# Turning the three-row maxima of an attention step by a transposing DMA instead of by TensorE

## The chip, the core and the metric

The kernel runs on one core of one Trainium2 chip. The metric is the device time of one execution in microseconds (us). Engines are named as in the profile: PE is TensorE (PEld its weight loads), DVE is VectorE, ACT is ScalarE, POOL is GpSimd, SP is SyncE, whose queue issues nearly all DMAs here. L560 means line 560 of the kernel before.

## The reference

An attention layer with a conditioning token and a residual. `x` is 8 x 512 x 512 (batch, sequence, model), with 16 heads of 32.

```python
Q = split_heads(x @ Wq.T + bq); K = ... Wk, bk; V = ... Wv, bv
tQ = split_heads(cond @ Wq.T + bq); tK = split_heads(cond @ Wk.T + bk)
scores = einsum('bhqd,bhkd->bhqk', Q + tQ, K + tK) / sqrt(32)
out = einsum('bhqk,bhkd->bhqd', softmax(scores), V)
return x + merge_heads(out)
```

All inputs and the output are float32.

## The kernel before, in words

**Steps.** The work is cut into 32 steps `t = 4*b + g` (T = 32): one batch `b` and one group `g` of four heads, whose 4 x 32 channels fill the 128 partitions. A step has four stages, and the loop at L796 writes out their order by hand for PE, ACT, DVE and POOL (a manual schedule), for t = 0 to 28. The last three steps have an order of their own (L904 onwards). The DMAs on SP are not in that manual schedule: the framework places them in SP's queue.

**Two passes over the scores.** A softmax needs the row maxima of the scores with queries on the partitions, but the probabilities are wanted with keys on the partitions, so that they can be multiplied with V without a transpose. So each step computes its scores twice. `row_max` (L482) has PE make scores with queries on partitions (L499), and DVE reduces them to negated maxima `nmax`, 128 x 4 x 4 (L490, L508). ACT then runs over the same scores once more for the sums of the exponentials (`denominators`, L518). Later `exponentials` (L555) has PE make the scores with keys on partitions (L563), with the negated maxima added in the same accumulation: L560 multiplies three rows of `maxT` by ones. ACT takes the exponential of that (L574).

**Three rows.** `maxT` holds, for each head, the negated maxima as three bfloat16 rows whose sum is the float32 value. `split_max` (L526) makes the three parts on POOL, in four small instructions (L532 to L535), into `split`, a 128 x 512 bfloat16 tile with the queries on partitions, used in turn from two buffers. `transpose_max` (L539) turns it: four PE transposes of 128 x 128 (L544) into one PSUM bank, and one copy from there into `maxT` (L550), which DVE does in the loop.

**Stages of iteration t.** Each begins with `exponentials(t, kc)` for one quarter `kc` of the keys, goes on with a `row_max` of the next step or, in the last stage, of the step after it, and ends with a share of other PE work:

- stage q: `row_max(t+1, 1)`, then a share of the q projection of the next batch (L406),
- stage w: `row_max(t+1, 2)`, then the probabilities times V of step t-1 (L579), and the result of step t-1 goes out by way of DVE (L635), POOL (L636, L637) and SP (L640),
- stage k: `row_max(t+1, 3)`, which completes the maxima of step t+1; `split_max(t+1)` on POOL; a share of the k projection; `load_residual(t+1)` (L165 on SP, L173 on POOL),
- stage v: `row_max(t+2, 0)`, then a share of the v projection (L403), in whose middle a callback `small` (L842) calls `transpose_max(t+1, ...)`.

The next iteration opens with `exponentials(t+1, 0)`, the first reader of `maxT[t+1]`. The letters q, w, k and v are used for the stages below.

**What orders the work.** Each engine runs its instructions in the written order; semaphores tie the engines together. PSUM has eight banks, dealt out to the stages by the table `TURNS`: per stage four banks for the exponentials (and then the projection), and four for the row maxima. Each transpose used one of these for a moment (index 1 or 2 of its stage). `split` has two buffers and `maxT` has two. On SP the DMAs of an iteration stand in this order: four loads of `x` blocks (L151), which wait for DVE; four stores of a result (L640), which wait for POOL's L637; four loads of a residual block (L165), one iteration ahead of their use.

Of the kernel before, what the change touches and what calls it, by code (L numbers as in the profile page):

```python
# [10 lines left out]
BF16 = mybir.dt.bfloat16  # L11
# [6 lines left out]
def kernel(  # L18
# [38 lines left out]
    nc = tc.nc  # L57
    P = 128
    B, S, D = x.shape
# [5 lines left out]
    NS = S // P  # L65
    NC = D // P
    SCALE = 1.0 / math.sqrt(HD)
    T = B * G
# [8 lines left out]
    op = ctx.enter_context(tc.tile_pool(name="op", bufs=2))  # L77
# [34 lines left out]
    def banks(i, n=1):  # L112

        j = TURNS[turn[0]][i]
        if n == 1:
            return psum[:, j, :]
        k = TURNS[turn[0]][i + 1]
        return psum[:, j : k + 1 : k - j, :]

    def advance():  # L120
        turn[0] = {7: 0, len(TURNS) - 1: 4}.get(turn[0], turn[0] + 1)
# [37 lines left out]
    def load_residual(t):  # L159

        b, g = divmod(t, G)
        if turned_by_vector(t):
            xr[t] = op.tile([P, NB, BL], F32, tag="xr", name=f"xr_{t}", bufs=3)
            for h in range(HG):
                nc.sync.dma_start(  # L165
                    xr[t][h * BL : (h + 1) * BL], spread(x[b], g * P + h * BL)
                )
            bias = bvs[:, g, :].unsqueeze(1).broadcast_to([P, NB, BL])
        else:

            xr[t] = xT[b][:, g, :]
            bias = bvl.broadcast_to([P, S])
        nc.gpsimd.tensor_tensor(xr[t], xr[t], bias, ALU.add)  # L173
# [62 lines left out]
    split = []  # L236
# [8 lines left out]
    for i in range(NS):  # L245
        r = slice(i * BL, (i + 1) * BL)
# [70 lines left out]
    def turn_x(n):  # L317
        b, cc = divmod(n, NC)
        if b >= B:
            return  # L320
        if cc == 0:
            xT[b] = xtp.tile([P, NC, S], F32, tag="xT", name=f"xT_{b}")
        nc.vector.transpose(xT[b][:, cc, :], xs[n].rearrange("p f i -> p (f i)"))
        load_block(n + NC)
# [106 lines left out]
    def first_products(n, b, u, dens, small, at, first=0):  # L431


        one_, two_ = banks(first), banks(at)
        c1, c12, c2, c22 = parts_of(n, b, u)
        m1 = c2[:, 0, :]
        product(n, b, u, 1, one_[:, :HS])
        nc.scalar.copy(m1, one_[:, :HS])
        dens()
        product(n, b, u, 6, two_[:, :HS])  # L440
        small()
        product(n, b, u, 2, two_[:, HS:], (0,))
        product(n, b, u, 7, one_[:, HS:])
        nc.vector.tensor_tensor(c12, two_[:, :HS], m1, ALU.add)
        nc.vector.tensor_tensor(c1[:, 0, :], two_[:, HS:], m1, ALU.add)
        plus(n, b, u, 1, c22, one_[:, HS:], c12)
# [18 lines left out]
    def project_pair(n, b, r, dens, small, at):  # L465

        if b >= B:
            dens()
            small()
        else:  # L470
            (first_products, other_products)[r % 2](n, b, r // 2, dens, small, at)
# [10 lines left out]
    def row_max(t, qc):  # L482
        if t >= T:
            return
        open_max(t)
        for j in range(HG):
            row_scores(t, qc, j, banks(HG + j))
        if t < T - 2 or t * NS + qc == T * NS - 1:
            for j in range(2):
                nc.vector.tensor_reduce(  # L490
                    nmax[t][:, qc, j : j + 1, 0], banks(HG + j), AX.X, ALU.max, negate=True
                )
        else:
            row_max_of(t, qc, 0, banks(HG, 2))
        row_max_of(t, qc, 1, banks(HG + 2, 2))
# [16 lines left out]
    def denominators(t, qc, prs=range(NP)):  # L512

        if t >= T - 2:
            return
        for j in [pr * 2 + i for pr in prs for i in range(2)]:
            dead = op.tile([P, S], F32, tag="dead", name=f"dead_{t}_{qc}_{j}")
            nc.scalar.activation(  # L518
                dead,
                banks(HG + j),  # L520
                AF.Exp,
                bias=nmax[t][:, qc, j, :],
                accum_out=sums[t][:, qc, j, :],
            )

    def split_max(t, on=nc.gpsimd):  # L526

        if t >= T:
            return
        m, sp = nmax[t], split[t % 2]  # L530
        rest = op.tile([P, NS, HG, 1], F32, tag="rest", name=f"rest_{t}")
        on.tensor_copy(sp[:, :, :, 0:1], m)  # L532
        on.tensor_tensor(rest, m, sp[:, :, :, 0:1], ALU.subtract)
        on.tensor_copy(sp[:, :, :, 1:2], rest)
        on.tensor_tensor(sp[:, :, :, 2:3], rest, sp[:, :, :, 1:2], ALU.subtract)  # L535

    maxT = {}

    def transpose_max(t, bank, copy=nc.vector.tensor_copy):  # L539
        if t >= T:  # L540
            return
        pt = bank.bitcast(BF16)
        for qc in range(NS):
            nc.tensor.transpose(  # L544
                pt[:, qc * P : (qc + 1) * P],
                split[t % 2][:, qc, :, :].rearrange("p h e -> p (h e)"),
                identb,
            )
        maxT[t] = op.tile([P, S], BF16, tag="maxT", name=f"maxT_{t}")
        copy(maxT[t], pt[:, :S])  # L550
# [4 lines left out]
    def exponentials(t, kc, at=None):  # L555

        bank = [psum[:, i, :] for i in at] if at else [banks(i) for i in range(HG)]
        for j in range(HG):
            r = slice(j * HD, j * HD + 3)
            nc.tensor.matmul(bank[j], onesb[r, :], maxT[t][r, :], start=True, stop=False)  # L560
        for j in range(HG):
            r = slice(j * HD, (j + 1) * HD)
            nc.tensor.matmul(  # L563
                bank[j],
                qkT["k", t][r, kc * P : (kc + 1) * P],
                qkT["q", t][r, :],
                start=False,
                stop=True,
            )
        for pr in range(NP):  # L570
            e = ep.tile([P, 2, S], F32, tag="e", name=f"e_{t}_{kc}_{pr}")
            es[t, kc, pr] = e
            for i in range(2):
                nc.scalar.activation(e[:, i, :], bank[pr * 2 + i], AF.Exp)  # L574
# [43 lines left out]
    def weighted(t, pt, pd, between):  # L618

        apart = masked(t)
        for kc in range(NS):
            times_v(t, kc, pt)
            if kc == 0:
                spread_sums(apart, pd)
        rec = op.tile([P, NB, 1], F32, tag="recs", name=f"recs_{t}")
        nc.vector.reciprocal(rec, pd[:, :NB].unsqueeze(2))
        between()
        send(t, pt, rec)  # L630
# [127 lines left out]
    advance()  # L758
    row_max(1, 0)
    transpose_max(0, banks(1), nc.scalar.copy)  # L760
    other_products("k", 0, 1, lambda: denominators(1, 0), nothing, (0, 2))
    turn_x(NC + 1)
# [33 lines left out]
    for t in range(T - 3):  # L796
        b, r = divmod(t, G)

        exponentials(t, 0)
        row_max(t + 1, 1)  # L800
        of = ((t - 1) // G + 1, (t - 1) % G)
        dens = lambda: denominators(t + 1, 1)
        if t:
            project_pair("q", *of, dens, nothing, 1 if r % 2 else (0, 3))
        else:
            first_products("v", 0, 0, dens, nothing, 1)
            turn_x(NC + 2)
            load_residual(1)
        turn_x(t + NC + 3)
        advance()  # L810

        exponentials(t, 1)
        row_max(t + 1, 2)
        dens = lambda: denominators(t + 1, 2)
        if t:
            dens()
            weighted(
                t - 1, banks(0), banks(1), lambda: combine_x(b + 1, r) if r < 2 else None
            )
        else:  # L820
            dens()
            other_products("v", 0, 0, nothing, nothing, (0, 2))
        advance()

        exponentials(t, 2)
        row_max(t + 1, 3)
        split_max(t + 1)
        dens = lambda: denominators(t + 1, 3)
        if t:
            project_pair("k", *of, dens, nothing, 1 if r % 2 else (0, 3))  # L830
        else:
            first_products("v", 0, 1, dens, nothing, 1)
            combine_x(1, 0)
        if t:
            load_residual(t + 1)
        advance()

        exponentials(t, 3)
        row_max(t + 2, 0)
        dens = lambda: denominators(t + 2, 0)  # L840

        def small():  # L842
            transpose_max(t + 1, banks(2 if r % 2 else 1))

        project_pair("v", *of, dens, small, 1 if r % 2 else (0, 2))
        advance()


# [55 lines left out]
    t = T - 3  # L904
# [21 lines left out]
    t = T - 2  # L926
# [24 lines left out]
    t = T - 1  # L951
# [103 lines left out]
```

## Time and profile before

| what | value |
|---|---|
| median of 3 runs | 729.93 us (729.53 to 730.05) |
| profiled execution, span from first to last instruction | 727.7 us |
| what lies around that span, against the median | 2.2 us |
| PE busy | 720.6 us (99%) |
| ACT busy | 616.6 us (85%) |
| DVE busy | 536.5 us (74%) |
| POOL busy | 175.9 us (24%) |
| DMA queue of SP (q1), packets and share of 16 engines | 205748, 22.5% |
| mean granted TensorE clock | 1.000 |

The profiled execution's own time is given as its span; the rest up to the median is what the device counts before the first and after the last instruction. A busy PE is not a PE at its peak: matmuls overlap, and their ends are modelled. So durations of PE work are best taken from one start to the next. Idle time of an engine that is not the bound costs nothing.

### The profile page before, as it was taken

What the parts mean: (1) busy time and instruction counts of PE and PEld (TensorE: products, weight loads), DVE (VectorE), ACT (ScalarE), POOL (GpSimd) and SP (SyncE); (2) the same over time, 40 slices, a digit from 0 to 9 for tenths busy, and PEclk for the clock granted to TensorE, in tenths of its full rate; (3) what the DMA queues carried; (4) which work ended last, traced back from release to release, by engine and by line L of the source; (5) the groups of instructions that cost most, each with busy time, mean ns of one, the idle gap of its engine ahead of it and who ended that gap; (6) DMA issues with size and microseconds to landing.
All of it is one profiled execution on the core that took longest, in us unless ns stands there. A gap on an engine that the chain in (4) does not pass through costs nothing.

```text
span 727.7 us, 15109 instructions
## 1 busy us (share of the span) xinstructions
PE 720.6 (99%) x5412; PEld 406.0 (56%) x5412; DVE 536.5 (74%) x863; ACT 616.6 (85%) x1539; POOL 175.9 (24%) x275
## 2 busy tenths in 40 slices
PE   9999999999999999999999999999999999999997
PEld 7566555566555566555566555565555565555532
DVE  4798777777768777678776877777767777767777
ACT  2589898899898898888899888888988989888664
POOL 3711221122221122221122221122221122221351
PEclk9999999999999999999999999999999999999999
DMA  6743221222221222221222221212110111110111
GB/s 176 110 64 49 45 45 23 38 39 36 44 44 21 40 34 40 45 41 23 42 33 41 44 40 22 44 31 43 31 23 9 31 29 31 30 20 11 30 31 29
DMA packets 207583, 29.12 MB, mean 40 GB/s; under 512 B 205834, under 2 KB 206346, under 8 KB 207508
## 3 DMA queue, kind: packets, MB, share of 16 engines
q1 hardware_dynamic: 205748, 27.11, 22.5%
q10 hardware_dynamic: 1760, 1.05, 0.5%
q8 instruction: 42, 0.69, 0.4%
q14 instruction: 33, 0.27, 0.1%
HBM read 19.75 MB, written 8.39 MB: 39 GB/s over the span
## 4 chain that ended last, share of the span: by engine, by line
PE 96%; DVE 2%; DMA 1%; issue 1%; DVEq 0%; SPq 0%
PE psum L406 27%; PE psum L499 16%; PE psum L579 15%; PE psum L403 14%; PE psum L563 14%; PE psum L560 5%; PE psum L350 2%; PE psum L544 1%; DVE acc L855 1%; DMA x<-in_x_dram 1%; PE psum L881 1%; PE psum L657 0%; DVE acc L853 0%; PE psum L589 0%; PE psum L266 0%
## 5 line engine op out<-in xcount | busy, mean ns | idle before, releaser
L518 ACT ACTIVATE dead<-psum,nmax 128x512 f32<-128x512 f32 x480 | 327.0, 701 | 5.2 <-DVE nmax L490 3.1
L574 ACT ACTIVATE e<-psum 128x512 f32<-128x512 f32 x488 | 251.9, 603 | 71.5 <-PE psum L563 71.2
L490 DVE TENSOR_REDUCE nmax<-psum 128x1 f32<-128x512 f32 x240 | 154.5, 685 | 142.8 <-PE psum L499 142.8
L508 DVE TENSOR_REDUCE nmax<-psum 128x2 f32<-128x1024 f32 x130 | 157.6, 1214 | 2.7 <-PE psum L499 2.7
L499 PE MATMUL psum<-kT,qT 32*128 32x512 f32 x1024 | 142.6, 601 | 0.0
L636 POOL TENSOR_TENSOR res<-res,recs 128x512 f32<-128x512 f32 x30 | 31.4, 1047 | 439.0 <-DVE res L635 439.0
L563 PE MATMUL psum<-qT,kT 32*128 32x512 f32 x976 | 125.5, 587 | 0.0
L579 PE MATMUL psum<-e,v 128*32 128x512 f32 x1024 | 121.2, 597 | 0.0
L518 ACT ACTIVATION_READ_ACCUMULATOR dead<-psum,nmax 128x1 f32 x480 | 104.8, 218 | 0.0
L499 PEld LDWEIGHTS psum<-kT,qT 32*128 32x128 f32 x1024 | 59.7, 183 | 57.1 <-ACT dead L518 19.6
L579 PEld LDWEIGHTS psum<-e,v 128*32 128x32 f32 x1024 | 26.6, 110 | 65.1 <-issue 37.6
L563 PEld LDWEIGHTS psum<-qT,kT 32*128 32x128 f32 x976 | 48.6, 185 | 2.2
L403 PE MATMUL psum<-wc_v,xc 128*128 128x256 f32 x192 | 49.3, 379 | 0.0
L560 PE MATMUL psum<-maxT,onesb 3*128 3x512 bf16 x488 | 48.2, 385 | 0.0
L406 PE MATMUL psum<-xc,wc_k 128*128 128x256 f32 x180 | 46.2, 379 | 0.0
L406 PE MATMUL psum<-xc,wc_q 128*128 128x256 f32 x180 | 46.2, 379 | 0.0
L560 PEld LDWEIGHTS <-onesb 3*128 3x128 bf16 x488 | 12.3, 91 | 57.2 <-issue 47.9
L173 POOL TENSOR_TENSOR xr<-xr,bvs 128x512 f32<-128x512 f32 x31 | 39.3, 1268 | 17.4 <-DMA xr<-in_x_dram 17.4
L403 PEld LDWEIGHTS psum<-wc_v,xc 128*128 128x128 f32 x192 | 36.5, 190 | 4.9
L403 PE MATMUL psum<-wT_v,xT 128*128 128x256 f32 x128 | 38.8, 405 | 0.0
L637 POOL TENSOR_TENSOR res<-res,xr 128x512 f32<-128x512 f32 x30 | 38.2, 1273 | 2.3
L406 PEld LDWEIGHTS psum<-xc,wc_q 128*128 128x128 f32 x180 | 34.2, 190 | 4.6
(165 smaller groups left out, 819.5 us busy)
## 6 DMA issues: line engine op xcount, KB each, us to landing
xr<-in_x_dram SPq DMA_DIRECT2D x124, 64.0 KB, 2.4
out_dram<-res SPq DMA_DIRECT2D x122, 64.0 KB, 1.9
x<-in_x_dram SPq DMA_DIRECT2D x112, 64.0 KB, 2.3
w_q<-in_L_cond_Wq_dram SPq DMA_DIRECT2D x4, 256.0 KB, 4.5
w_v<-in_L_cond_Wv_dram SPq DMA_DIRECT2D x16, 64.0 KB, 2.4
w_k<-in_L_cond_Wk_dram SPq DMA_DIRECT2D x16, 48.0 KB, 2.6
x<-in_x_dram ACTq DMA_DIRECT2D x2, 256.0 KB, 3.9
x<-in_x_dram SPq DMA_DIRECT2D x2, 256.0 KB, 4.1
```

Of the source, the lines that this page charges most:

```text
L173: nc.gpsimd.tensor_tensor(xr[t], xr[t], bias, ALU.add)
L403: nc.tensor.matmul(pt, xb, w, start=(kc == kcs[0]), stop=(kc == kcs[-1]))
L406: nc.tensor.matmul(pt, w, xb, start=(kc == kcs[0]), stop=(kc == kcs[-1]))
L490: nc.vector.tensor_reduce(nmax[t][:, qc, j : j + 1, 0], banks(HG + j), AX.X, ALU.max, negate=True)
L499: nc.tensor.matmul(pt, qkT["q", t][r, qc * P : (qc + 1) * P], qkT["k", t][r, :], start=True, stop=True,)
L508: nc.vector.tensor_reduce(nmax[t][:, qc, pr * 2 : pr * 2 + 2, 0], pt, AX.X, ALU.max, negate=True)
L518: nc.scalar.activation(dead, banks(HG + j), AF.Exp, bias=nmax[t][:, qc, j, :], accum_out=sums[t][:, qc, j, :],)
L560: nc.tensor.matmul(bank[j], onesb[r, :], maxT[t][r, :], start=True, stop=False)
L563: nc.tensor.matmul(bank[j], qkT["k", t][r, kc * P : (kc + 1) * P], qkT["q", t][r, :], start=False, stop=True,)
L574: nc.scalar.activation(e[:, i, :], bank[pr * 2 + i], AF.Exp)
L579: nc.tensor.matmul(pt[j * HD : (j + 1) * HD, :], vs[b % 2][:, kc, (g * HG + j) * HD : (g * HG + j + 1) * HD], es[t, kc, j // 2][:, j % 2, ...
L637: nc.gpsimd.tensor_tensor(y, y, xr.pop(t), ALU.add)
```

## The change

For steps 1 to 29 the four PE transposes and DVE's copy are taken out of stage v. In their place one DMA, issued on SP, moves `split` to `maxT` from SBUF to SBUF and transposes on the way. It is called directly after `split_max(t+1)`, in stage k. Steps 0, 30 and 31 are turned by PE as before.

```diff
+    def turn_max(t):
+
+        if t >= T:
+            return
+        maxT[t] = op.tile([P, S], BF16, tag="maxT", name=f"maxT_{t}")
+        nc.sync.dma_start_transpose(
+            maxT[t].rearrange("p (c q) -> p c q", c=NS),
+            split[t % 2].rearrange("p c h e -> p (c h e)"),
+        )
...
         exponentials(t, 2)
         row_max(t + 1, 3)
         split_max(t + 1)
+        turn_max(t + 1)
...
         row_max(t + 2, 0)
         dens = lambda: denominators(t + 2, 0)
 
-        def small():
-            transpose_max(t + 1, banks(2 if r % 2 else 1))
-
-        project_pair("v", *of, dens, small, 1 if r % 2 else (0, 2))
+        project_pair("v", *of, dens, nothing, 1 if r % 2 else (0, 2))
         advance()
```

In the order that the framework gives SP's queue, the new DMA of an iteration (from step 2 on) stands behind the four result stores and the first of the four residual loads, and ahead of the other three. On PE it is waited for by the first weight load of `exponentials(t+1, 0)`, the one ahead of L560.

## The prediction

> **What bounds the kernel now.** I read the busy shares first, then the chain that ended last, then the instructions in order of time over two iterations in mid-span, PE's first, and last POOL and SP around the moved work. From the page, PE's and the DMA engines' busy tenths, and the chain by engine:
>
> ```profile
> PE   9999999999999999999999999999999999999997
> ...
> DMA  6743221222221222221222221212110111110111
> ...
> PE 96%; DVE 2%; DMA 1%; issue 1%; DVEq 0%; SPq 0%
> ```
>
> PE is on the chain for 96% of the span, and the DMA engines are mostly idle. So work taken off PE counts in full as long as nothing late makes PE wait. PE's instructions in order of time (start, length, line, tiles, count):
>
> ```profile
> 301.04 0.59 PE L406 MATMUL psum<-xT,wT_k 128*128 128x256 f32 x2
> 301.47 1.03 PE L406 MATMUL psum<-xc,wc_k 128*128 128x256 f32 x4
> 302.43 0.39 PE L560 MATMUL psum<-maxT,onesb 3*128 3x512 bf16 x4
> 302.66 1.03 PE L563 MATMUL psum<-qT,kT 32*128 32x512 f32 x8
> 303.52 1.11 PE L499 MATMUL psum<-kT,qT 32*128 32x512 f32 x8
> 304.56 1.13 PE L403 MATMUL psum<-wT_v,xT 128*128 128x256 f32 x4
> 305.53 1.03 PE L403 MATMUL psum<-wc_v,xc 128*128 128x256 f32 x4
> 306.40 0.39 PE L544 MATMUL psum<-identb,split 128*128 128x128 bf16 x4
> 306.62 0.65 PE L403 MATMUL psum<-wT_v,xT 128*128 128x256 f32 x2
> 307.11 1.03 PE L403 MATMUL psum<-wc_v,xc 128*128 128x256 f32 x4
> 308.07 0.39 PE L560 MATMUL psum<-maxT,onesb 3*128 3x512 bf16 x4
> ```
>
> The reader is to see the end of a stage k, then a whole stage v, with no gap. Start to start, L544 takes 306.62 - 306.40 = 0.22 us, and the L403 behind it 0.49 where the same place in stage k takes 0.43 (301.04 to 301.47). Stage v lasts 5.64 us; stages q and k, with the same number of products, last 5.26 to 5.29 everywhere in the trace. So a stage v costs 0.37 us more than its like. Of this 0.28 lie at the transposes (0.22 + 0.06). The other 0.08 lie at L499, which takes 1.04 from its start to the next (303.52 to 304.56) where stage q shows 0.96: its first weight load waits there for DVE's kT, just written, which this change leaves alone. The other parity of iteration gives 0.23 and 0.05.
>
> Now the supply. POOL and SP in order of time, same iteration:
>
> ```profile
> 302.76 0.27 POOL L535 TENSOR_TENSOR split<-rest,split 128x16 bf16<-128x16 f32 x1
> ...
> 300.58 1.97 SPq L640 DMA_DIRECT2D out_dram<-res  x4
> 302.59 2.10 SPq L165 DMA_DIRECT2D xr<-in_x_dram  x4
> 314.89 1.91 SPq L151 DMA_DIRECT2D x<-in_x_dram  x4
> ```
>
> `split` is complete at 303.03. The stores are issued by then, and SP has nothing to do from 304.69 to 314.89.
>
> **Removed.** 29 x 4 transposes on PE: 29 x 0.28 = 8.1 us, on the path. If the 0.08 at L499 went too, it would be 29 x 0.37 = 10.7; I don't count it. 29 copies on DVE (L550, 413 ns): in stage v DVE runs without a gap from 304.64 to 308.59, so its evictions behind the copy move forward with PE's products. DVE is 74% busy and PE does not wait for it at the next stage's start, so beyond keeping step this is worth nothing. One PSUM bank per stage is left by ACT earlier, which can only help.
>
> **Does the saving pass through the other engines?** With PE 0.28 earlier, the next L560 would start at 307.79 and the next L499 at 308.87. L499 needs the banks that ACT's denominators leave; ACT runs from 303.71 to 308.79 without a gap and is tied to the start of stage v, not to its end. So 0.08 us of slack remain; with a signal's delay I allow at most 0.05 lost in every second iteration, 0.7 us in all. ACT then still idles some 0.3 us before its next exponential (0.56 before).
>
> **Added: one DMA per step, and PE's wait for it.** It waits on SP for POOL's L535 (303.03). Ahead of it stand four stores, issued at 302.55, and one residual load, issued from 302.59 to about 303.08 (487 ns for one, the median of L165). So it starts on SP at 303.08. PE wants it at 307.79. The cover is 4.70 us; in the other parity it is issued at 324.95 and wanted at 329.92 - 0.28 = 329.64, which is 4.69.
>
> How long from issue to landing? No transposing DMA stands in this trace. The nearest rows are the DMAs of the same queue (KB each, median us from issue to landing):
>
> ```profile
> out_dram<-res SPq DMA_DIRECT2D x122, 64.0 KB, 1.9
> x<-in_x_dram SPq DMA_DIRECT2D x112, 64.0 KB, 2.3
> ...
> w_q<-in_L_cond_Wq_dram SPq DMA_DIRECT2D x4, 256.0 KB, 4.5
> ```
>
> A 64 KB transfer is 512 pieces of 128 bytes. The new one is 128 x 512 bfloat16 (128 KB): 128 rows of four 256-byte pieces, again 512 pieces if they stay whole. Lower bound: a store's 1.9 us. Upper bound: all pieces one after another instead of over 16 engines. Queue q1 shows 22.5% x 16 x 727.7 us / 205748 packets = 12.7 ns of an engine per packet, so 512 x 12.7 = 6.5 us, plus 1.9, is 8.4. (Split into its 65536 elements it would be far beyond that, 52 us even over 16 engines; I give this next to no chance.) I take 3 us: it is nearest to the 64 KB rows in pieces and queue, between these and the 256 KB row, which itself stays under 4.70. Residual load traffic is beside it: in stage v the DMA share is 0.44, and I count that within the 3 us.
>
> The Trainium skill speaks against the change here. Its page "VectorE: DVE Perf Modes", section "The three transpose paths", gives a 128 x 128 bfloat16 transpose 1309 ns through the DMA and 390 ns on TensorE. Four of the former in a row would be an estimated 5.24 us, 0.54 more than the cover, and by that the sum would be 29 x 0.54 - 8.1 = 7.6 us slower, 737.5. No row of this trace shows whether four blocks in one DMA cost four times one; the row of TensorE is 0.22 us for four, start to start, far below the page's figure. The page "Advanced Engine Details and Errata", section "X-Bar Transpose (TRN2)", holds the opposite, that transposing DMAs are as fast as ordinary ones; by that the stores' row would do, and the landing would be hidden with room.
>
> **Queued behind it on SP:** three residual loads, then `x` loads and stores. SP is idle until 314.89, so the transpose may hold SP for (314.89 - 303.08) less 1.6 us for the three loads, 10 us, before the `x` loads move. The residual loads are used by POOL's L173 an iteration later (the L173 at 302.95 starts before this iteration's loads can have landed), so some 20 us later. Cost: nothing. On PE everything queues behind the waiting weight load: a late landing is paid by PE in full, and ACT and DVE wait behind it.
>
> **Sum.** 729.93 - 8.1 + 0 to 0.7 gives 721.8 to 722.5; I say 722.0. Against the profiled execution: 727.7 - 7.9 = 719.8, plus the 2.2 us around it.
>
> **Rivals.**
> 1. *The landing is late (slower).* Place: PE's first weight load of `exponentials(t+1, 0)`. It decides from a landing of 4.70 + 0.28 = 4.98 us. Price: 29 us for every us beyond 4.70, less 8.1. At 6 us: +29.6, 759.5; at the bound of 8.4: +99, 829. For it: the 256 KB row at 4.5, and loads in flight on the same rings. Against: the 64 KB rows have medians of 1.9 to 2.4, and the longest single one is 4.1.
> 2. *The saving is absorbed.* L499 of the next stage waits for ACT's denominators, whose margin is 0.08. If ACT is later than read, half or all of it goes: 726 to 730. Against: ACT idles 0.26 to 0.86 us in each stage.
> 3. *The 0.08 goes as well:* 729.93 - 10.7 = 719.2. For it: stage v would become like q and k. Against: the wait named there is for kT.
> That the change doesn't do what it says is excluded: the built order has 29 transposing DMAs on SP and 232 fewer rows on PE.
>
> **How the numbers follow.** Hidden landing (722.0, with rival 3 as its lower edge): 0.70. Rival 1: 0.22. Rival 2: 0.08, more than half of it within 0.2% (1.5 us, about what a measurement can tell). So faster 0.72, same 0.05, slower 0.23. Likeliest case alone: 719 to 723.5. For 8 in 10 the range takes in rival 2 and about a third of rival 1, up to a landing of 5.25 us: 29 x 0.55 - 8.1 = +7.9, 737.8. So 718.8 to 738.
>
> **What would show it.** Right: stage v at about 5.35 us; no idle PE weight load released by a DMA ahead of L560; landing under 4.7; SP's `x` loads unmoved against their stage; ACT idle shorter. Wrong: PE weight loads ahead of L560 that name the DMA of maxT as releaser, 29 times; a stage v over 5.64; a transposing DMA that holds SP for microseconds. What would make the prediction wrong above all is the landing, the one number that I had no row for.

## The result, and the profile after

The changed kernel takes 722.5 us (median of 4 runs, 722.21 to 722.59), beside 729.99 us for the kernel before on the same chip: a ratio of 0.990, with a 95% interval of 0.9887 to 0.9913. That is 7.5 us less; 722.0 was forecast. The profiled execution's span goes from 727.7 to 720.8 us, 6.9 less.

In the changed kernel the lines named here from L539 on have numbers higher by 10: L570 is the old L560 (ones times `maxT`), L573 the old L563, L584 the old L574, L589 the old L579, L650 the old L640, L554 the old L544. The transposing DMA is L544.

The page of the changed kernel, the chain by engine:

```profile
PE 97%; DVE 2%; issue 1%; DMA 1%; DVEq 0%
```

PE is still the chain, and no new engine has come into it. PE's order in time, one stage v up to the start of the stage q behind it (start, length):

```profile
321.63 0.40 PE L570 MATMUL psum<-maxT,onesb 3*128 3x512 bf16 x4
...
322.72 1.11 PE L499 MATMUL psum<-kT,qT 32*128 32x512 f32 x8
323.76 1.13 PE L403 MATMUL psum<-wT_v,xc 128*128 128x256 f32 x4
...
325.59 0.59 PE L403 MATMUL psum<-wT_v,xT 128*128 128x256 f32 x2
326.02 1.03 PE L403 MATMUL psum<-wc_v,xT 128*128 128x256 f32 x4
326.98 0.39 PE L570 MATMUL psum<-maxT,onesb 3*128 3x512 bf16 x4
```

The four products of the v projection now follow one another without the transposes, and the third takes 0.43 us to the next start, as in the other stages. Stage v lasts 326.98 - 321.63 = 5.35 us; in both kinds of step it went from 5.63 to 5.35. L499 still takes 1.04 (322.72 to 323.76), so the 0.08 us of waiting there have stayed.

The supply, POOL and SP in order of time around the same stage:

```profile
321.94 0.27 POOL L535 TENSOR_TENSOR split<-rest,split 128x16 bf16<-128x16 f32 x1
...
321.81 0.49 SPq L165 DMA_DIRECT2D xr<-in_x_dram  x1
322.40 1.19 SPq L544 DMA_TRANSPOSE maxT<-split  x1
...
333.70 1.91 SPq L151 DMA_DIRECT2D x<-in_x_dram  x4
```

The DMA is issued 0.19 us after `split` is complete (the median of the 29), and holds SP for 1.19 us. Its reader, the L570 at 326.98, comes 4.58 us after the issue. The same by tile (lowest, median and highest; 18 of the 29 landings are on record):

```profile
L544 SPq DMA_TRANSPOSE maxT<-split x29: 1188/1188/2249, 62.3 to 668.9; - x29
...
DMA to landing us min/median/max: 2.4/2.5/2.8
```

So 2.1 us of cover are left over in the usual step. PE's list of waits in this trace names no DMA of `maxT` ahead of L570. A second trace of the same kernel (run a_same below) has one step of 29 in which the data came later: the DMA was issued at 452.11, and PE's weight load waited for it until 456.91, 4.80 us after the issue. That stage v lasts 5.56 us instead of 5.35.

```profile
456.91 0.10 PEld L570 LDWEIGHTS <-onesb 3*128 3x128 bf16 x4 [0.54 <-DMA maxT<-split]
```

The saving is not passed on whole. Behind one of the two kinds of step (odd and even), stage q lasts 5.35 us where it lasted 5.26. One such stage q in the changed kernel:

```profile
305.32 0.40 PE L570 MATMUL psum<-maxT,onesb 3*128 3x512 bf16 x4
...
310.67 0.40 PE L570 MATMUL psum<-maxT,onesb 3*128 3x512 bf16 x4
```

Its weight loads for L499, first before (in the stage q from 308.07 to 313.33, 5.26 us), then after:

```profile
308.73 0.62 PEld L499 LDWEIGHTS psum<-kT,qT 32*128 32x128 f32 x8 [0.24 <-issue]
```

```profile
306.38 0.30 PEld L499 LDWEIGHTS psum<-kT,qT 32*128 32x128 f32 x7 [0.22 <-ACT dead L518]
```

After the change, all but the first of these loads start only at 306.38, 0.05 us after ACT's last L518 of the stage before has ended (306.33). There are 14 such new waits. In PE's list of waits, L499 stands behind ACT's L518 60 times before, 74 times in a_same and 89 times in the first trace. The other 15 of those 89 lie in stages w that kept their 5.68 us; before and in a_same the same idle time is listed under "issue", that is, as a wait for nothing that the profile shows.

The sum, from starts to starts: 29 x 0.28 = 8.1 us less in stages v, 14 x 0.08 = 1.1 us more in stages q, 7.0 together, against 6.9 of span.

### The profile page after: what moved, and what is told of

It reads as the page before. It is cut to its first block, busy times and chain, and to the rows that moved or that the text cites. A ratio compares the mean times of both kernels' runs of the same rounds, so it can differ in the third digit from the quotient of the medians.

```text
span 720.8 us, 14892 instructions
## 1 busy us (share of the span) xinstructions
PE 714.2 (99%) x5296; PEld 401.3 (56%) x5296; DVE 528.0 (73%) x834; ACT 617.3 (86%) x1539; POOL 176.3 (24%) x275
## 3 DMA queue, kind: packets, MB, share of 16 engines
q1 hardware_dynamic: 221524, 30.92, 25.3%
## 4 chain that ended last, share of the span: by engine, by line
PE 97%; DVE 2%; issue 1%; DMA 1%; DVEq 0%
PE psum L406 27%; PE psum L499 16%; PE psum L589 15%; PE psum L403 14%; PE psum L573 14%; PE psum L570 5%; PE psum L350 2%; DVE acc L863 1%; PE psum L889 1%; DMA w_q<-in_L_cond_Wq_dram 1%; PE psum L266 0%; DVE acc L861 0%; PE psum L311 0%; PE psum L667 0%; PE psum L599 0%
## 5 line engine op out<-in xcount | busy, mean ns | idle before, releaser
L518 ACT ACTIVATE dead<-psum,nmax 128x512 f32<-128x512 f32 x480 | 327.6, 702 | 5.1 <-DVE nmax L490 3.1
L584 ACT ACTIVATE e<-psum 128x512 f32<-128x512 f32 x488 | 252.0, 602 | 64.2 <-PE psum L573 63.9
L499 PE MATMUL psum<-kT,qT 32*128 32x512 f32 x1024 | 143.9, 605 | 0.0
L573 PE MATMUL psum<-qT,kT 32*128 32x512 f32 x976 | 125.5, 587 | 0.0
L589 PE MATMUL psum<-e,v 128*32 128x512 f32 x1024 | 121.2, 596 | 0.0
L518 ACT ACTIVATION_READ_ACCUMULATOR dead<-psum,nmax 128x1 f32 x480 | 105.2, 219 | 0.0
L499 PEld LDWEIGHTS psum<-kT,qT 32*128 32x128 f32 x1024 | 59.8, 183 | 58.1 <-ACT dead L518 26.4
L589 PEld LDWEIGHTS psum<-e,v 128*32 128x32 f32 x1024 | 26.6, 110 | 65.1 <-issue 37.6
L573 PEld LDWEIGHTS psum<-qT,kT 32*128 32x128 f32 x976 | 48.6, 185 | 2.2
L570 PE MATMUL psum<-maxT,onesb 3*128 3x512 bf16 x488 | 48.1, 384 | 0.0
L570 PEld LDWEIGHTS <-onesb 3*128 3x128 bf16 x488 | 12.3, 90 | 57.2 <-issue 57.2
L403 PE MATMUL psum<-wT_v,xT 128*128 128x256 f32 x128 | 37.1, 392 | 0.0
L406 PEld LDWEIGHTS psum<-xc,wc_k 128*128 128x128 f32 x180 | 34.2, 190 | 4.7
```

The lines of the kernel that those rows point to most:

```text
L403: nc.tensor.matmul(pt, xb, w, start=(kc == kcs[0]), stop=(kc == kcs[-1]))
L406: nc.tensor.matmul(pt, w, xb, start=(kc == kcs[0]), stop=(kc == kcs[-1]))
L499: nc.tensor.matmul(pt, qkT["q", t][r, qc * P : (qc + 1) * P], qkT["k", t][r, :], start=True, stop=True,)
L518: nc.scalar.activation(dead, banks(HG + j), AF.Exp, bias=nmax[t][:, qc, j, :], accum_out=sums[t][:, qc, j, :],)
L573: nc.tensor.matmul(bank[j], qkT["k", t][r, kc * P : (kc + 1) * P], qkT["q", t][r, :], start=False, stop=True,)
L589: nc.tensor.matmul(pt[j * HD : (j + 1) * HD, :], vs[b % 2][:, kc, (g * HG + j) * HD : (g * HG + j + 1) * HD], es[t, kc, j // 2][:, j % 2, ...
```

## The experiments

The theory at the start was the prediction's: the gain is PE's time, and the DMA is hidden with some 2 us to spare. The rivals: the gain comes from DVE's copy or its bank; the DMA is close to being late; the loss in stage q has another cause than ACT.

### PE's transposes put back beside the DMA (e1, e1b)

```diff
+        def small():
+            if t + 1 < T:
+                pt = banks(2 if r % 2 else 1).bitcast(BF16)
+                for qc in range(NS):
+                    nc.tensor.transpose(
+                        pt[:, qc * P : (qc + 1) * P],
+                        split[(t + 1) % 2][:, qc, :, :].rearrange("p h e -> p (h e)"),
+                        identb,
+                    )
-        project_pair("v", *of, dens, nothing, 1 if r % 2 else (0, 2))
+        project_pair("v", *of, dens, small, 1 if r % 2 else (0, 2))
```

> The four PE transposes of a step are done again in stage v, into the same bank, and nobody reads them; the transposing DMA stays and feeds maxT; the DVE copy stays away. Reading of the prediction (the gain is PE's time): stage v goes back from 5.35 to about 5.63 us, 29 x 0.28 = 8.1 us come back, less the 0.08 us that every second stage q loses now: 729 to 730 us, ratio to before 0.999 to 1.001. Rival (the gain comes from the DVE copy or from the bank that it held): 722.5 to 724, ratio 0.99.

Measured: 729.16 us, ratio to before 0.9993 (0.9984 to 1.0003). The same kernel was run again for a trace:

> e1 once more, for a trace of it. New theory after e2 (PE's transposes and DVE's copy each hold most of the gain back by themselves): stage v at 5.6 us again in both kinds of step, and stage q at 5.26 to 5.27 in both, since PE's own length covers DVE and ACT: 728.5 to 729.5 us. If e1's time came from something else than stage v: stage v at 5.35 us.

Measured: 729.3 us, ratio 0.9999 (0.9989 to 1.0009). PE's order in time in e1b (L857 are the transposes that nobody reads):

```profile
324.77 0.40 PE L570 MATMUL psum<-maxT,onesb 3*128 3x512 bf16 x4
...
328.73 0.39 PE L857 MATMUL psum<-identb,split 128*128 128x128 bf16 x4
328.95 0.65 PE L403 MATMUL psum<-wT_v,xT 128*128 128x256 f32 x2
...
330.40 0.39 PE L570 MATMUL psum<-maxT,onesb 3*128 3x512 bf16 x4
```

Stage v is at 5.63 us again, the whole gain is gone, and stage q is at 5.26 to 5.27 behind both kinds of step. So taking away DVE's copy and its use of a bank, with PE's transposes still there, and having the DMA in its place, is together worth nothing.

### A copy on DVE put back, without PE's transposes (e2, e2b)

```diff
+        def small():
+            gone = op.tile([P, 384], F32, tag="gone", name=f"gone_{t}", bufs=1)
+            nc.vector.tensor_copy(gone, banks(2 if r % 2 else 1)[:, :384])
-        project_pair("v", *of, dens, nothing, 1 if r % 2 else (0, 2))
+        project_pair("v", *of, dens, small, 1 if r % 2 else (0, 2))
```

> As the changed kernel, with a DVE copy of 128x384 float32 out of the old bank put back in the middle of stage v (about 0.4 us, into a tile that nobody reads), and no PE transposes. Reading of the prediction: DVE keeps step behind PE, so 722.5 to 723.5 us, ratio 0.990 to 0.991. Rival (the copy was what paced stage v): stage v back at about 5.6 us and 728 to 730 us.

Measured: 728.26 us, ratio 0.9984 (0.9975 to 0.9994). That is neither as the prediction had it nor as the rival did. Stage v stays at 5.35 us, but stage q goes from 5.26 to 5.64 behind the other kind of step, the one that lost nothing by the change. The copy took 548 ns, longer than the one that was removed (413 ns), so e2b has 256 columns in place of 384:

> As e2, with a copy of 128x256 float32, about 415 ns, as long as the copy that the change removed (413 ns). New theory after e2 (DVE's evictions at the end of stage v of every second step come so late that the scores of the next stage q wait for their banks): they end about 0.13 us earlier than in e2, so every second stage q has about 0.13 us less of its 0.38 us excess: 14.5 x 0.25 = 3.6 us over the changed kernel, about 726 us. If the copy's own length is not what matters, but that there is one more instruction and one more user of the bank: 728 us as in e2. Reading of the prediction (the copy is free): 722.5 us.

Measured: 725.89 us (ratio to before 0.995, 0.9937 to 0.9962), beside 722.33 us for the changed kernel on the same chip. The copy is now 416 ns. 3.6 us come back, as the new theory had it. In e2b, DVE and PE in order of time at the end of such a stage v and in the stage q behind it:

```profile
327.25 0.42 DVE L855 COPY gone<-psum 128x256 f32<-128x256 f32 x1
...
328.01 0.40 PE L570 MATMUL psum<-maxT,onesb 3*128 3x512 bf16 x4
328.51 0.68 DVE L426 TENSOR_TENSOR v<-psum,v 128x512 f32<-128x512 f32 x1
329.10 1.27 PE L499 MATMUL psum<-kT,qT 32*128 32x512 f32 x8
...
330.30 1.13 PE L406 MATMUL psum<-xT,wT_q 128*128 128x256 f32 x4
```

L426, the last of DVE's three evictions, ends at 329.19, 1.18 us after L570 started. L499 starts 1.09 us after L570, and not all of its four heads find their banks free: the fourth head's first product starts at 329.25, 0.06 us after the end of L426 and 0.14 us behind the other three. L499 takes 1.20 us to the next start instead of 0.95. In the changed kernel the same L426 runs from 327.15 to 327.83, only 0.85 us after its L570 at 326.98, and L499 is not held. So in these steps DVE was right behind PE: once PE is 0.28 us shorter, a copy of the old length would have been the next limit.

### Delaying the landing (e4, e5, e5b)

One, two or three transposing DMAs of the same tile, which nobody reads, are issued directly ahead of the real one (e4 shown):

```diff
+        for i in range(1):
+            gone = op.tile([P, S], BF16, tag=f"gone{i}", name=f"gone_{t}_{i}", bufs=1)
+            nc.sync.dma_start_transpose(
+                gone.rearrange("p (c q) -> p c q", c=NS),
+                split[t % 2].rearrange("p c h e -> p (c h e)"),
+            )
         maxT[t] = op.tile([P, S], BF16, tag="maxT", name=f"maxT_{t}")
```

> One more transposing DMA of the same tile, into a tile that nobody reads, is issued on SP directly ahead of the real one, so that it starts about 1.23 us later. Cover is about 4.6 us from the start of the first. Reading of the prediction: landing at 1.23 + 2.5 = 3.7 us is still hidden: 722.5 to 723 us, but for the two steps with a late store. Rival (two transposes in flight share what limits them, or the landing is nearer to the edge than the trace says): PE weight loads ahead of the first product with maxT wait, 0.5 us or more per step, 737 us or more.

> Two more transposing DMAs ahead of the real one, which starts some 2.46 us later and would land 2.46 + 2.5 = 4.96 us after the start of the first. Reading of the prediction: late by about 0.36 to 0.4 us against a cover of 4.58: 29 x 0.38 = 11 us, so 733 to 734 us, slower than the kernel before, with a DMA named ahead of PE's weight load. Rival (the wait is absorbed, since PE makes up for it later in the iteration): 723 to 726.

> Three more transposing DMAs ahead of the real one, which starts some 3.69 us later and would land 6.2 us after the start of the first. Reading of the prediction (29 us for every us beyond the cover of 4.58): late by 1.6 us, 29 x 1.6 = 46 us, so about 769 us (765 to 773). Rival (part of the wait is made up later in the iteration): 745 to 760.

| kernel | time, us | ratio to before | real DMA issued after `split`, median / mean | L576 after `split`, mean |
|---|---|---|---|---|
| changed kernel (its L570) | 722.5 | 0.990 (0.9887 to 0.9913) | 0.19 / 0.30 | 4.77 |
| one ahead | 725.50 | 0.9941 (0.9924 to 0.9958) | 1.45 / 1.58 | 4.88 |
| two ahead | 748.41 | 1.028 (1.0235 to 1.0325) | 2.79 / 2.95 | 5.63 |
| three ahead | 790.05 | 1.0818 (1.0787 to 1.0848) | 4.08 / 4.32 | 6.86 |

The last two columns are worked out from the starts in the traces, in us (L576 is the old L560 in these kernels; stage v's own start is 0.6 us before `split` is complete). The direction and the edge are as expected: one ahead is nearly hidden, two ahead is late in every step. PE's list of waits with two ahead:

```profile
PEld L576 <- DMA maxT<-split: 34.7, 29, 2.4
```

Wherever PE waits for it, L576 starts 2.47 to 2.50 us after the issue in most steps, so this is the usual time from issue to use. The sizes were underestimated, by 3, 15 and 21 us, for two reasons that the traces show. First, each DMA ahead costs 1.30 us on SP, not 1.23. Second, now and then a DMA on SP takes 0.2 to 1.5 us longer than its kind: 10 to 12 of them in the steady part of each of these runs, the kernel before included. When one falls between `split` and the real issue, the issue is late: 2.65 and 2.69 us after `split` in two of the seven late steps with one ahead. In the other five the issue is on time (1.43 to 1.55), and the data are used 3.55 to 4.42 us after it instead of 2.5. In four of these the real DMA, or the one behind it on SP, is itself one of the long ones. With two ahead the shortest step starts at 5.21 and the median one at 5.33, but the mean is 5.63, and (5.63 - 4.77) x 29 = 25 us is the loss of 26. With three ahead, (6.86 - 4.77) x 29 = 61 of 67.5 us; the rest has to do with the clock: four stages q last 1.6 to 2.9 us longer (below).

So the price of 29 us per us of lateness holds, for the mean lateness. Next to nothing of it is made up later: with two ahead all stages q are back at 5.26, which returns the 1.1 us that they had lost.

### Four small DMAs instead of one (e6)

```diff
-        nc.sync.dma_start_transpose(
-            maxT[t].rearrange("p (c q) -> p c q", c=NS),
-            split[t % 2].rearrange("p c h e -> p (c h e)"),
-        )
+        for c in range(NS):
+            nc.sync.dma_start_transpose(
+                maxT[t][:, c * P : (c + 1) * P],
+                split[t % 2][:, c, :, :].rearrange("p h e -> p (h e)"),
+            )
```

> The one DMA of 128x512 is cut into four of 128x128. If SP's time for it (1.19 us) is a fixed cost of each DMA: the fourth starts 3.7 us after the first and lands at 6.0 to 6.2 us, 1.5 us late, 29 x 1.5 = 43 us: 760 to 770 us. If it goes by the bytes: four of 0.3 us, and the time stays at 722.5 to 723.5 us. With the figure of the Trainium skill (page VectorE: DVE Perf Modes, The three transpose paths: 1309 ns for 128x128) as the time that each takes of the queue, an estimated 4 x 1.31 = 5.2 us to the last landing, 0.6 us late, 740 us.

Measured: 781.75 us, ratio 1.0696 (1.0662 to 1.0731). The transposing DMAs of e6, by tile:

```profile
L545 SPq DMA_TRANSPOSE maxT<-split x116: 1093/1230/2428, 61.9 to 732.2; - x116
```

A DMA of 128x128 holds SP for 1.23 us, one of 128x512 for 1.19: it is a cost of each DMA and doesn't go by the bytes at these sizes. The fourth is issued 3.88 us after `split` (median), and PE starts 2.48 us after that issue, 1.8 us late on the mean: 53 us. The rest again has to do with the clock, and takes the time above the 760 to 770 that were expected.

This settles the rule that spoke against the change. The Trainium skill's 1309 ns for a 128x128 block through the DMA ("VectorE: DVE Perf Modes", "The three transpose paths") is near the time that one DMA holds SP here, 1.23 us, but four blocks in one DMA do not cost four times that.

### The DMA on ACT's queue (e8)

```diff
         split_max(t + 1)
-        turn_max(t + 1)
...
+        turn_max(t + 1)
         if t:
             load_residual(t + 1)
...
-        nc.sync.dma_start_transpose(
+        nc.scalar.dma_start_transpose(
```

> The transposing DMA is issued by ACT instead of SP, at the end of stage k, after ACT's denominators and ahead of the exponentials of stage v. If the issue holds ACT as it holds SP, 1.19 us per step: ACT idles 0.25 us there, so the exponentials start 0.9 us late; PE waits for their banks in stage v or q, and of ACT's 1.2 to 1.4 us of idle time per iteration all is used up: 735 to 755 us. If issuing costs ACT next to nothing: 722.5 us.

Measured: 736.53 us, ratio 1.0095 (1.008 to 1.011). ACT in order of time in e8:

```profile
305.90 1.21 ACTq L544 DMA_TRANSPOSE maxT<-split  x1
...
307.16 1.09 ACT L584 ACTIVATE e<-psum 128x512 f32<-128x512 f32 x2 [0.85 <-PE psum L573]
```

The issue holds ACT's queue for 1.21 us, up to 307.11, and the exponentials start right behind it, at 307.16; their releaser in brackets is the data, not what held them. Stage v goes from 5.35 to 5.75, and one stage q in two from 5.35 to 5.48: 29 x 0.40 + 14 x 0.13 = 13.4 us of the 14 lost against the changed kernel. So the same DMA gains 7.5 us on the idle queue and loses 7 on a busy one.

### An attempt on the 0.08 us of stage q (e7, e9)

```diff
+    swap = {4: 6, 5: 7, 6: 4, 7: 5}
+    first = len(TURNS)
+    for row_ in TURNS[:8]:
+        TURNS.append(tuple(swap.get(j, j) for j in row_))
+
     def advance():
-        turn[0] = {7: 0, len(TURNS) - 1: 4}.get(turn[0], turn[0] + 1)
+        turn[0] = {7: first, first + 7: 0, first - 1: 4}.get(turn[0], turn[0] + 1)
```

e9 has, besides, `turn_max(t + 1)` behind the `split_max(t + 1)` of the last steps' order, in place of step 30's `transpose_max`.

> The changed kernel once more, as the base for the next three on the same chip: ratio to before 0.990, 722.5 us.

> The changed kernel with the PSUM banks 4, 5 and 6, 7 exchanged in every second round of eight stages, so that stage q behind an odd step's stage v computes its first two scores in the banks that DVE has left, and the last two in those that ACT's denominators leave last. If the 0.08 us that every second stage q lost with the change (5.35 instead of 5.27) is the wait for ACT's last denominators: it goes in 14 stages, 1.1 us, about 721.4 us, ratio 0.15% under the changed kernel's. If it is something else: 722.5 us.

> e7 and, besides, step 30's maxima turned by the DMA too, issued on SP after its split. Reading of the prediction: 0.28 us of PE for the four transposes, and up to 0.8 us of a wait of PE's weight loads at that place, if the landing (2.5 us after an issue at about 685.5 us, wanted at about 688.2 us) comes in time: 0.3 to 1.0 us under e7, 720.5 to 721.2 us.

Measured: the changed kernel 722.33 us (ratio to before 0.9899, 0.9886 to 0.9913), e7 730.46 us (1.0011, 1.0002 to 1.002), e9 730.09 us (1.0009, 1.0 to 1.0017). The exchange of banks loses 8.1 us against the changed kernel. In seven places, once in each exchanged round, a stage k lasts 5.49 us instead of 5.26 and the stage v behind it 6.29 instead of 5.35, 8 us in all. ACT and PE at such a place in e7:

```profile
213.70 0.69 ACT L523 ACTIVATE dead<-psum,nmax 128x512 f32<-128x512 f32 x1 [1.04 <-DVE nmax L513]
...
215.20 0.39 PE L575 MATMUL psum<-maxT,onesb 3*128 3x512 bf16 x3 [0.30 <-ACT dead L523]
```

There the first denominators of stage k wait 1.04 us for DVE's second reduction (L513), which they don't need, and PE pays for it at the start of the next stage. In that row the exchange makes the second pair of banks 3 and 6, which spans banks 4 and 5; that the dependence comes from there fits the row of the table, but wasn't tried by itself. The stage q that was meant to gain went from 5.35 to 5.33 only. Its last score still needs the bank that ACT leaves last, wherever it stands in the order. So the time neither confirms nor excludes that ACT's chain is the cause of the 0.08. The starts of the products speak for it: each head has two in L499, and in the changed kernel the second comes 1.52 us after the stage's start for the first head and 1.60 for the other three, in e7 1.52 for three heads and 1.59 for the fourth alone. By the table, the bank that ACT leaves last is the second head's in the changed kernel and the fourth head's in e7: the delay has moved with that bank. Step 30 by the DMA is worth 0.3 us by the trace: in the order of the last steps, from an L891 (ones times `maxT` there; 691.63 in e7, 691.20 in e9) to the next L575 (706.38 and 705.68), 14.75 us become 14.48. The 0.37 us between the two medians is smaller than either's interval. No version tried is faster than the changed kernel.

## Why the prediction was right, and where not

- **What bounds the kernel.** Right. PE's order from start to start gave 0.28 us per step, and the traces show 5.63 to 5.35; e1b gives it back whole. Rival 3 (0.37) fell: the 0.08 at L499 stayed. But the wait for kT, which was named against it, is only part of the reason. In the very stage that the prediction shows, two loads wait for kT and the six behind them for ACT's last L518, which ends at 303.45 (lines below, from before the change). In the other kind of step kT does come last (325.20, ACT at 325.11). That none of the 0.08 would go was right; that it hung on kT holds for half of the steps.

```profile
303.09 0.19 PEld L499 LDWEIGHTS psum<-kT,qT 32*128 32x128 f32 x2 [0.24 <-DVE kT L429]
303.51 0.30 PEld L499 LDWEIGHTS psum<-kT,qT 32*128 32x128 f32 x6 [0.23 <-ACT dead L518]
```

- **What does not pass through.** The place, L499 of the next stage q, and what it waits for, ACT's denominators, were right. It was allowed to lose up to 0.05 us in every second iteration, 0.7 us; it lost 0.08, 1.1 us. The margin of 0.08 was taken from ACT's end to PE's product (308.79 to 308.87), but what waits is the weight load ahead of the product, which started 0.05 us after ACT's end and takes 0.18. This is the one term of the sum that was too small, and it makes most of the 0.5 us between 722.0 and 722.5.
- **DVE's copy: "worth nothing".** True by itself (e1b), but the step missed what it holds up: with the copy in place only about half of PE's saving would have come through (e2b, 725.9 us). The forecast was right because both went together. That is luck: for the transposes alone, the same reading would have forecast a time some 3.6 us too short. The prediction read DVE in the kind of step where it ends at 308.59, well before L499. In the other kind, before the change, DVE's last eviction ends at 330.82, 0.90 us after the start of L560, and the fourth head's weight load for L499 starts right behind it, at 330.88 (line below, from before the change).

```profile
330.14 0.68 DVE L426 TENSOR_TENSOR v<-psum,v 128x512 f32<-128x512 f32 x1
```

- **The landing.** 3 us were taken, between rows of 1.9 and 4.5; 2.5 was measured. The pieces stayed whole: SP's queue has 221524 packets instead of 205748, 544 more for each DMA. The cover was 4.58 instead of 4.70, since some 0.1 us pass on SP between one issue and the next. Hidden, by 2.1 us in the usual step; the one use after 4.80 us in a_same shows that this is no margin for every step.
- **SP.** The transpose holds SP for 1.19 us, far under the 10 us that were free. The `x` loads keep their place. Not foreseen were the single long issues on SP. Two of them delayed a transpose in the changed kernel to 1.22 and 1.45 us after `split`, which left 3.5 and 3.3 us of cover, still enough.
- **Rival 1** had the right place and price. Its edge stands where `split` is followed by the issue more than some 2.3 us later. That is two more such DMAs ahead of it.

## What to carry to other kernels

A small transfer is free where it is issued early, on a queue that is idle, and read late. Compare its time from issue to use (2.48 us here in most steps, up to 4.8 in single ones) with the span between the two ends, and then look at what else holds that queue. An engine that is 99% busy hands its saving on only as far as the next engine's slack goes: for each instruction removed, ask which other engine ran without a gap in that stage, and put the removed parts back one at a time, since one of them may be worth nothing by itself (the copy here) and still hold back half of what the other is worth. Count a transposing DMA by the DMA and not by the byte while it is this small, and never put its issue on an engine that is itself near the path.

## What the runs showed of the hardware that was not expected

- The time for which a transposing DMA holds its queue does not depend on its size between 128x128 (1.23 us) and 128x512 bfloat16 (1.19 us). It is 2.4 times that of an ordinary 64 KB DMA (0.49), on ACT's queue (1.21) as on SP's.
- Single DMAs on SP are held up by 0.2 to 1.5 us, 8 to 13 times per run, in the kernel before and in the versions with the transposes on SP, at nearly the same times in different kernels (near 129, 299 and 454 us in the changed kernel and in e4). No view shows what they wait for.
- After PE had stood still for 2 to 3 us, TensorE's granted clock sometimes fell to half for 3.41 us, or once for 6.83. In e5b this followed 4 of the 29 gaps, in e6 some 7. PE and then the window (length, busy time by engine, granted clock) of one such place in e6:

```profile
185.49 0.40 PE L571 MATMUL psum<-maxT,onesb 3*128 3x512 bf16 x4 [2.01 <-DMA maxT<-split]
```

```profile
185.46:192.41 6.95, 6.92 (x34) 3.86 (x34) 3.18 (x5) 4.18 (x10) 0.00 (x0) 0.75 0.14 21
```

The stage q behind the gap lasts 6.92 us instead of 5.34. Gaps of the same length elsewhere in these runs (up to 3.09 us) left the clock alone, so the length alone does not decide it. The Trainium skill ("TensorE: Matmul & The Clock Gate", Part 1) tells of a monitoring window of 3413 ns that runs freely. The traces agree, and they show its phase: between any two changes of the clock within a trace lie whole multiples of 3.413 us (139.95 us in e6, for one, are 41 of them). Divide e5b and e6 at these points, from 60 us to behind the last gap: by the profile's ends of products (which are modelled) the clock went to half after each of the 11 windows in which PE stood still for 1.93 us or more in all, and after none in which it stood still for 1.80 or less. The gap of 3.09 us fell on two windows, with 1.45 and 1.64 us. In the changed kernel the clock stays at full speed up to its last microseconds.
